# Two of the seven products of an opening block product cut by a third Strassen-Winograd step, with the routing projection's second quarter set between their pieces

## The chip, the cores and the metric

The kernel runs on one core of one Trainium2 chip. Its time is device time in microseconds (us). The program ran three times: 428.74, 428.77 and 429.66 us, median 428.77. One more execution was taken by the hardware profiler; every start and duration below is from that one. A difference of less than 0.2% (0.86 us) is not told apart from none.

TensorE (PE in the profile) multiplies matrices into PSUM. VectorE (DVE) adds and subtracts, ScalarE (ACT) copies, GpSimd (POOL) and SyncE (SP) hardly compute.

## The reference

All in float32. Layer 0 adds to `x` a dense product and a gated low-rank term, layer 1 adds a product with a weight matrix chosen by the row of the batch:

```python
# x: (8, 256, 1024)
base = einsum('btd,od->bto', x, W)                 # 1024 x 1024 weights
logits = einsum('btd,ed->bte', x, Wr) + bias       # 8 experts, +5 for the language's own
topw, topi = top_k(logits, 2)
gates = sum(one_hot(topi, 8) * softmax(topw)[..., None], -2)
h = einsum('btd,erd->bter', x, A)                  # 8 experts of rank 16
x = x + base + 2.0 * einsum('bter,bte,eor->bto', h, gates, B)
x = x + einsum('bsi,boi->bso', x, weight[adapter_ids])
```

The identity is added to the weight matrices, which makes the residual sums part of the products.

## The kernel before, in words

**Layer 0** is a product of 1024x1024 weights with 1024x2048 tokens, by two nested steps of the Strassen-Winograd scheme: seven block products instead of eight, each of which again is seven of eight smaller ones. A block product (keys "1" to "7") has weights `wb` and tokens `xb` of four quadrants each, `a(i, j)` (256x256) and `b(i, j)` (256x512). Its seven smaller products P1 to P7 need sums and differences of quadrants, made on DVE: `s1` to `s3` of the weights and `t1` to `t3` of the tokens; late in the product `s2` and `t2` are overwritten by a further difference (`late`). One smaller product is four matmuls of 128x128 weights with 128x512 tokens (`mm`, line 447), each of which is two records in the profile. Results gather in PSUM tiles A, B and X, and go out by an ACT copy or by a DVE sum onto what is there already (`evict`, line 435; every DVE sum and difference has line 217).

**A third step** exists in `product`, for its smaller product P2 alone: there, seven 128x256 matmuls (`deep`, line 513), called pieces here, stand for the four. Its own small sums are `r1` to `r4` (128x128) and `q1` to `q4` (128x256); `r1`, `r3` share a buffer, and so do `q1`, `q3`. Pieces 1, 6 and 7 are added up one after the other in one PSUM bank, and after each of them the bank's content is taken out; piece 5 has a bank of its own; pieces 2, 3 and 4 add straight onto a tile that gathers.

**PSUM**[...] three pairs (tags pair0, pair1, pair2) and two singles.

**The opening** is block product "1". It has a function of its own, `opening`, since it runs while inputs still arrive. Between its smaller products stand parts of the **projection** (`project`, line 245): tokens times the 136 columns of `A` and `Wr`, 32 matmuls of 128x136 for each of four quarters (two halves j of the tokens, two of each half c). The first quarter is (0, 0). A quarter is eight chunks, one for each 128 of the contraction, with four matmuls in each. `take` brings a quarter out: for each of two banks a DVE sum for the logits and an ACT copy for h.

The last smaller products of the opening are P7 (`mm(A, t["s3"], t["t3"])`), P3 (`mm(B, t["s2"], b(1, 1))`, onto B, then a DVE sum) and P4 (`mm(A, a(1, 1), t["t2"])`, onto A, then an ACT copy).

**The order around the change** is written out by hand[...]. After the opening, DVE makes differences of the low-rank B (`b_differences`), adds the identity to a weight block, makes two weight sums and `s1`, `s2` of product "5"; then comes the second quarter, `project(1, 0)`, and its take, four differences of x (`t1`), the third quarter `project(1, 1)` and its take, the gating of the half 1 (`gating`, some twenty small operations on DVE and one on ACT, last a product of the gates onto h), the other four differences of x, the fourth quarter `project(0, 1)`, the transposes of the gated h (`turn`, line 315), and product "5". Later products hand out DVE work between their matmuls from a list (`todo`, `pump`).

**Layer 1** handles eight batch rows, one adapter each, with one Strassen-Winograd step (`adapt`, line 660); loads of the weights run through SP's queue.

Of the kernel before, what the change touches and what calls it, by code (L numbers as in the profile page):

```python
# [25 lines left out]
def kernel(  # L26
# [335 lines left out]
        return pieces(fn, wb[out_], wb[x], wb[y], 2)  # L362

    subs = {}

    def make_subs(key, w, x, further=True):

        def a(i, j):  # L370
            return wb[w][:, 2 * j : 2 * j + 2, i * OQ : (i + 1) * OQ]

        def b(i, j):
            return xb[x][:, 2 * i : 2 * i + 2, j * TQ : (j + 1) * TQ]


        ra = lambda i, j: a(0, 1)[:, j, ts(i, P)]
        rb = lambda i, j: b(1, 0)[:, i, ts(j, TQ // 2)]
        t = {}

        def op3(name, tag, fn, x, y, first=4):
            width = P if name[0] == "r" else TQ // 2

            def run():
                t[name] = sub3.tile([P, width], F32, name=f"{name}_{key}", tag=tag)
                fn(t[name], *(t[v] if isinstance(v, str) else v for v in (x, y)))

            return us(width), first, run

        deep = [  # L390
            op3("r1", "r13", add, ra(1, 0), ra(1, 1)),
            op3("q1", "q13", minus, rb(0, 1), rb(0, 0)),
            op3("r2", "r2", minus, "r1", ra(0, 0)),
            op3("q2", "q2", minus, rb(1, 1), "q1"),
            op3("r4", "r4", minus, ra(0, 1), "r2"),
            op3("q4", "q4", minus, rb(1, 0), "q2"),
        ]

        def deep3():
            for o in (  # L400
                op3("r3", "r13", minus, ra(0, 0), ra(1, 0)),
                op3("q3", "q13", minus, rb(1, 1), rb(0, 1)),
            ):
                o[2]()

        def op(name, fn, x, y, first):
            pool = sub2 if name[1] == "2" else sub1
            width = OQ if name[0] == "s" else TQ

            def run():  # L410
                t[name] = pool.tile([P, 2, width], F32, name=f"{name}_{key}", tag=name)
                fn(t[name], *(t[v] if isinstance(v, str) else v for v in (x, y)))

            return us(2 * width), first, run

        def late_s():
            minus(t["s2"], a(0, 1), t["s2"])

        def late_t():
            minus(t["t2"], b(1, 0), t["t2"])  # L420

        subs[key] = (a, b, t, (late_s, late_t), (ra, rb, deep3), further)
        return [
            op("s1", add, a(1, 0), a(1, 1), 3),
            op("t1", minus, b(0, 1), b(0, 0), 3),
            op("s2", minus, "s1", a(0, 0), 3),
            op("t2", minus, b(1, 1), "t1", 3),
            op("s3", minus, a(0, 0), a(1, 0), 5),
            op("t3", minus, b(1, 1), b(0, 1), 5),
        ] + (deep if further else [])  # L430

    def evict(dest, acc, base=None):

# [24 lines left out]
    def opening(key, dest):  # L458


        idle = pair("idle", 2)
        for i in range(WARM):
            nc.tensor.matmul(idle[:, 0, :P], lhsT=ident, rhs=ident, start=True, stop=True)  # L463
        mm = multiply()
        sums_of = make_subs(key, "11", "11", False)
        a, b, t, late, _, _ = subs.pop(key)
        X = pair(f"X_{key}", 0)
        A = pair(f"A_{key}", 1)
        add_identity(wb["11"], 0, 2)
        mm(X, a(0, 1), b(1, 0), True, part=(0,))  # L470
        project(0, 0, singles("ps_h_0_0"), (2,), last=False)
        mm(X, a(0, 1), b(1, 0), part=(1,))
        evict(dest[:, 0], X)
        project(0, 0, None, (3,), False, False)
        mm(A, a(0, 0), b(0, 0), True, part=(0,))
        project(0, 0, None, (0,), False, False)
        mm(A, a(0, 0), b(0, 0), part=(1,))
        project(0, 0, None, (1,), False, False)
        use_adapter_ids()
        add_identity(wb["11"], 2, 4)  # L480
        for s in sums_of[:4]:
            s[2]()
        add(dest[:, 0], A, dest[:, 0])
        nc.tensor.matmul(idle[:, 1, :NB], lhsT=ones, rhs=ids_f[:, :NB], start=True, stop=True)
        use_ids(idle[:, 1, :NB])
        B = pair(f"B_{key}", 2)
        mm(B, t["s1"], t["t1"], True)
        evict(dest[:, 3], B)
        for s in sums_of[4:]:
            s[2]()  # L490
        mm(A, t["s2"], t["t2"])
        evict(dest[:, 1], A)
        project(0, 0, None, range(KH, KC), False)
        take(0, 0)
        for f in late:
            f()
        mm(A, t["s3"], t["t3"])
        add(dest[:, 3], A, dest[:, 3])
        mm(B, t["s2"], b(1, 1))
        add(dest[:, 1], B, dest[:, 1])  # L500
        mm(A, a(1, 1), t["t2"])
        evict(dest[:, 2], A)

    def product(key, base, dest, lora=None, tokens=None):

        a, b, t, late, (ra, rb, deep3), further = subs.pop(key)
        mm = multiply(dict(zip("01d", b_part(lora))) if lora is not None else None, tokens)
        new = roles(key)
        old = [base[:, q] if base is not None else None for q in range(4)]
        n0, n1 = (slice(j * (TQ // 2), (j + 1) * (TQ // 2)) for j in range(2))  # L510

        def deep(acc, lhs, rhs, first=False):
            nc.tensor.matmul(acc, lhsT=lhs, rhs=rhs, start=first, stop=True, skip_group_check=True)  # L513

        def quarter(m, n):

            return dest[:, 0][:, m, n], old[0][:, m, n] if base is not None else None

        A = new("A")
        mm(A, a(0, 0), b(0, 0), True)  # L520
        X = new("X")
        nc.scalar.copy(X, A)
        if not further:
            pump(1)
            B = new("B")
            mm(B, t["s1"], t["t1"], True, "1", 1)
            evict(dest[:, 3], B, old[3])
            pump(3)
            mm(A, t["s2"], t["t2"])
            evict(dest[:, 1], A, old[1])  # L530
            pump(3)
            mm(X, a(0, 1), b(1, 0), False, "0", 0)
            late[0]()
            late[1]()
            evict(dest[:, 0], X, old[0])
            pump(4)
            mm(A, t["s3"], t["t3"])
            add(dest[:, 3], A, dest[:, 3])
            pump(5)
            mm(B, t["s2"], b(1, 1), False, "d", 1)  # L540
            add(dest[:, 1], B, dest[:, 1])
            pump(6)
            mm(A, a(1, 1), t["t2"], False, "1", 0)
            evict(dest[:, 2], A, old[2])
            pump(7)
            return
        A3 = single(f"A3_{key}", 0)[:, n0]
        deep(A3, ra(0, 0), rb(0, 0), True)
        q, o = quarter(0, n0)
        evict(q, A3, o)  # L550
        pump(1)
        B = new("B")
        mm(B, t["s1"], t["t1"], True, "1", 1, ms=(0,))
        B3 = single(f"B3_{key}", 1)[:, n0]
        deep(B3, t["r1"], t["q1"], True)
        deep3()
        mm(A, t["s2"], t["t2"])
        evict(dest[:, 1], A, old[1])
        deep(A3, t["r2"], t["q2"])
        q, o = quarter(0, n1)  # L560
        evict(q, A3, o)
        late[0]()
        pump(2)
        mm(B, t["s1"], t["t1"], True, "1", 1, ms=(1,))
        evict(dest[:, 3], B, old[3])
        late[1]()
        pump(3)
        deep(X[:, 0, n0], ra(0, 1), rb(1, 0))
        deep(X[:, 0, n1], t["r4"], rb(1, 1))
        deep(X[:, 1, n0], ra(1, 1), t["q4"])  # L570
        mm(X, None, None, False, "0", 0, part=())
        deep(A3, t["r3"], t["q3"])
        two = [P, 2, TQ // 2]
        d1 = dest[:, 0][:, 1, :].rearrange("p (j n) -> p j n", j=2)
        both = A3.unsqueeze(1).to_broadcast(two)
        evict(d1, both, old[0][:, 1, :].rearrange("p (j n) -> p j n", j=2) if base is not None else None)
        add(dest[:, 0][:, :, n1], B3.unsqueeze(1).to_broadcast(two), dest[:, 0][:, :, n1])
        add(dest[:, 0], X, dest[:, 0])
        pump(4)
        mm(A, t["s3"], t["t3"])  # L580
        add(dest[:, 3], A, dest[:, 3])
        pump(5)
        mm(B, t["s2"], b(1, 1), False, "d", 1)
        add(dest[:, 1], B, dest[:, 1])
        pump(6)
        mm(A, a(1, 1), t["t2"], False, "1", 0)
        evict(dest[:, 2], A, old[2])
        pump(7)
# [176 lines left out]
    subs5 = make_subs("5", "21", "12")  # L765
    subs5[0][2]()
    subs5[2][2]()
    project(1, 0, halves(pair("ps_h_1_0", 0)))
    take(1, 0)

    def t1(c, k):
# [102 lines left out]
```

## Time and profile before

| | |
|---|---|
| median of three runs | 428.77 us |
| the profiled execution's own time | 430.16 us |
| its span (first to last instruction) | 428.4 us |
| PE busy | 423.1 us, 99%, 1246 records |
| weight loads (PEld) | 217.3 us, 51% |
| DVE busy | 281.7 us, 66%, 375 instructions |
| ACT busy | 39.6 us, 9%, 65 instructions |
| granted TensorE clock | 0.999 of full speed |
| DMA | 55.83 MB, mean 130 GB/s |
| P3 of the opening starts on PE | 31.48 us |
| second quarter of the projection starts on PE | 38.34 us |
| transposes start on PE | 60.58 us |

A line of the timeline has the start, the length from the first start to the last end, engine, source line, operation, the tile written, the tiles read, their shape and how many instructions are merged in it. Brackets give how long the engine had been idle, and what ended that. Where instructions are merged, the time of one follows from the difference of two starts rather than from a record's length, since matmul records overlap. A tile's name in the profile is that of the buffer: `y` holds the results and, early on, also the logits, gates and h; `x`, `w` are inputs; `s`, `t`, `r`, `q` the sums.

### The profile page before, as it was taken

Reading aid. Unit: us, or ns where it says so; the run is one execution under the profiler, and the core shown is the slowest. Engines: PE = TensorE matmul, PEld = TensorE weight load, DVE = VectorE, ACT = ScalarE, POOL = GpSimd, SP = SyncE. Lnnn points to the kernel's source line nnn. Section 1 sums busy time; section 2 is a strip of 40 time slices with the busy share of each in tenths; the row PEclk is TensorE's granted clock in tenths of the full one; section 3 lists DMA queues with packets and bytes.
Section 4 is the critical chain, followed back from the end, with each engine's and each line's share of the span. In section 5 each row is a group of like instructions: output and inputs, shape, how many; then the busy total and the mean of one; then the engine's idle time right before and its main releaser. Section 6 shows DMA issues by size and latency. Waiting matters only on the chain.

```text
span 428.4 us, 3335 instructions
## 1 busy us (share of the span) xinstructions
PE 423.1 (99%) x1246; PEld 217.3 (51%) x1246; DVE 281.7 (66%) x375; ACT 39.6 (9%) x65; POOL 2.0 (0%) x10
## 2 busy tenths in 40 slices
PE   8999999999999999999999999999999999999996
PEld 5566984545444445444454444444444444444574
DVE  1627288956988959889595676565756576565531
ACT  1120022110000000000000101010110101010110
POOL 1000000000000000000000000000000000000000
PEclk9999999999999999999999999999999999999999
DMA  8995000000000140630302276556748385550202
GB/s 279 383 398 217 2 0 2 0 0 2 0 0 0 31 168 0 249 142 0 99 0 98 98 262 227 199 207 208 272 148 313 128 275 214 196 197 0 98 2 99
DMA packets 14305, 55.83 MB, mean 130 GB/s; under 512 B 1232, under 2 KB 3536, under 8 KB 9808
## 3 DMA queue, kind: packets, MB, share of 16 engines
q1 hardware_dynamic: 12976, 54.68, 35.5%
q10 hardware_dynamic: 1248, 0.93, 0.7%
q8 instruction: 10, 0.16, 0.2%
q14 instruction: 7, 0.06, 0.0%
q0 software_dynamic: 64, 0.00, 0.0%
HBM read 47.22 MB, written 8.39 MB: 130 GB/s over the span
## 4 chain that ended last, share of the span: by engine, by line
PE 98%; DVE 0%; POOL 0%; issue 0%; ACT 0%; POOLq 0%; DVEq 0%
PE A L447 24%; PE A L660 22%; PE B L447 14%; PE B L660 13%; PE ps_h L245 7%; PE X L660 6%; PE X L447 4%; PE A_last L718 3%; PE A L513 1%; PE X L513 1%; PE idle L463 1%; PE ps_g L315 0%; PE B L513 0%; DVE y L217 0%; ACT z L748 0%
## 5 line engine op out<-in xcount | busy, mean ns | idle before, releaser
L660 PE MATMUL B<-x,x 128*128 128x512 f32 x128 | 57.5, 592 | 0.0
L447 PE MATMUL A<-t,s 128*128 128x512 f32 x112 | 50.3, 592 | 0.0
L217 DVE TENSOR_TENSOR y<-A,y 128x1024 f32<-128x1024 f32 (+2 forms) x27 | 26.3, 985 | 25.1 <-PE A L447 14.2
L660 PE MATMUL A<-w,x 128*128 128x512 f32 x88 | 39.6, 592 | 0.0
L660 PEld LDWEIGHTS B<-x,x 128*128 128x128 f32 x128 | 24.3, 190 | 29.8 <-issue 29.7
L217 DVE TENSOR_TENSOR w<-w,w 128x1024 f32<-128x1024 f32 x24 | 29.0, 1223 | 15.4 <-PE A L660 15.3
L660 PE MATMUL A<-w,y 128*128 128x512 f32 x88 | 39.1, 592 | 0.0
L447 PEld LDWEIGHTS A<-t,s 128*128 128x128 f32 x112 | 21.2, 190 | 22.9 <-issue 22.5
L245 PEld LDWEIGHTS ps_h<-y,x 128*128 128x128 f32 x256 | 30.7, 191 | 3.3 <-issue 3.3
L245 PE MATMUL ps_h<-y,x 128*128 128x136 f32 x256 | 30.6, 279 | 0.0
L660 PEld LDWEIGHTS A<-w,x 128*128 128x128 f32 x88 | 16.7, 190 | 21.0 <-issue 21.0
L660 PEld LDWEIGHTS A<-w,y 128*128 128x128 f32 x88 | 16.7, 190 | 21.0 <-issue 21.0
L435 ACT COPY z<-A 128x512 f32<-128x512 f32 x21 | 12.3, 586 | 158.3 <-PE A L660 158.3
L447 PE MATMUL B<-t,s 128*128 128x512 f32 x56 | 25.9, 594 | 0.3 <-DVE bias L200 0.3
L447 PE MATMUL A<-x,w 128*128 128x512 f32 x56 | 25.3, 592 | 0.0
L447 PE MATMUL A<-t,w 128*128 128x512 f32 x56 | 25.2, 592 | 0.0
L447 PE MATMUL B<-x,s 128*128 128x512 f32 x56 | 25.2, 592 | 0.0
L217 DVE TENSOR_TENSOR y<-B,y 128x1024 f32<-128x1024 f32 (+1 forms) x16 | 17.4, 1090 | 9.5 <-PE B L447 8.7
L217 DVE TENSOR_TENSOR x<-x,x 128x1024 f32<-128x1024 f32 (+1 forms) x20 | 19.2, 1004 | 0.0
L447 PEld LDWEIGHTS B<-x,s 128*128 128x128 f32 x56 | 10.6, 190 | 13.4 <-issue 12.7
L447 PEld LDWEIGHTS A<-t,w 128*128 128x128 f32 x56 | 10.6, 190 | 13.4 <-issue 12.7
L217 DVE TENSOR_TENSOR z<-X,z 128x512 f32<-128x512 f32 x8 | 5.5, 692 | 17.9 <-PE X L660 15.9
(119 smaller groups left out, 446.3 us busy)
## 6 DMA issues: line engine op xcount, KB each, us to landing
x<-w_dram SPq DMA_DIRECT2D x24, 1024.0 KB, 4.8
w<-w_dram SPq DMA_DIRECT2D x8, 1024.0 KB, 4.8
out_dram<-z SPq DMA_DIRECT2D x15, 512.0 KB, 3.0
x<-xT_dram SPq DMA_DIRECT2D x6, 1024.0 KB, 12.9
w<-wT_dram SPq DMA_DIRECT2D x3, 1024.0 KB, 14.9
x<-xT_dram SPq DMA_DIRECT2D x4, 256.0 KB, 3.8
x<-xT_dram SPq DMA_DIRECT2D x2, 512.0 KB, 7.4
w<-w11T_dram SPq DMA_DIRECT2D x1, 512.0 KB, 6.1
```

Source lines behind the costliest of these rows:

```text
L217: nc.vector.tensor_tensor(out_, x, y, op)
L245: nc.tensor.matmul(ps[v][:, u * EA : (u + 1) * EA], lhsT=xk(k, j, c)[:, ts(r, P)], rhs=aw_sb[:, k, :], start=(first and k == some[0] and u ...
L435: nc.scalar.copy(dest, acc)
L447: nc.tensor.matmul(acc[:, m, :], lhsT=l, rhs=r, start=(first and i < len(ms)), stop=(i >= len(steps) - len(ms)), skip_group_check=True,)
L463: nc.tensor.matmul(idle[:, 0, :P], lhsT=ident, rhs=ident, start=True, stop=True)
L513: nc.tensor.matmul(acc, lhsT=lhs, rhs=rhs, start=first, stop=True, skip_group_check=True)
L660: nc.tensor.matmul(accs[name], lhsT=lhs[:, k // 2, k % 2, :], rhs=rhs[:, k, :], start=(first and k == 0), stop=(k == KH - 1), skip_group_c ...
L718: nc.tensor.matmul(acc, lhsT=lhs[:, k // 2, k % 2, :], rhs=rhs[:, k, ts(v, m)], start=(first and k == 0), stop=(k == KH - 1), skip_group_c ...
```

## The change

The code of the third step moves out of `make_subs` and `product` into one function, `third`, which gives back the small sums, the late small sums (`ops3`), a function for a piece and one for taking a bank out (`take`, called `out` in the opening). `product` uses it and keeps its order of work. In `opening`, P3 and P4 are each cut into seven pieces. The second quarter of the projection moves from behind the weight sums into the opening: its eight chunks stand between the pieces. P3's results are added by DVE onto the quadrant that is there; P4's pieces 1, 6 and 7 are copied by ACT, its piece 5 and the tile A are added by DVE, where P4 was one ACT copy before. P3's first small sums stand before the second late difference (`t2`) on DVE. The pieces use the two single banks, the quarter uses pair0.

```diff
+    def third(key, lhs, rhs):
+        ra = lambda i, j: lhs()[:, j, ts(i, P)]
+        rb = lambda i, j: rhs()[:, i, ts(j, NQ)]
...
+        def ops3():
+            op("r3", "r13", minus, A(0, 0), A(1, 0))[2]()
+            op("q3", "q13", minus, B(1, 1), B(0, 1))[2]()
+
+        def piece(n, acc=None):
+            if n in (1, 5):
+                own[n] = single(f"P{n}_{key}", n // 5)[:, n0]
+            out_, l, r = {
+                1: lambda: (own[1], ra(0, 0), rb(0, 0)),
+                2: lambda: (acc[:, 0, n0], ra(0, 1), rb(1, 0)),
+                3: lambda: (acc[:, 0, n1], t["r4"], rb(1, 1)),
+                4: lambda: (acc[:, 1, n0], ra(1, 1), t["q4"]),
+                5: lambda: (own[5], t["r1"], t["q1"]),
+                6: lambda: (own[1], t["r2"], t["q2"]),
+                7: lambda: (own[1], t["r3"], t["q3"]),
+            }[n]()
+            nc.tensor.matmul(out_, lhsT=l, rhs=r, start=(n in (1, 5)), stop=True, skip_group_check=True)
+
+        def take(n, dest, base=None):
+            cut = lambda v: {1: v[:, 0, n0], 6: v[:, 0, n1], 5: v[:, :, n1]}[n]
+            if n == 7:
+                cut = lambda v: v[:, 1, :].rearrange("p (j n) -> p j n", j=2)
+            src = own[5 if n == 5 else 1]
+            if n in (5, 7):
+                src = src.unsqueeze(1).to_broadcast([P, 2, NQ])
+            evict(cut(dest), src, None if base is None else cut(base))
...
     def opening(key, dest):
...
         take(0, 0)
-        for f in late:
-            f()
+        late[0]()
+        ops, ops3, piece, out = third(f"{key}b", lambda: t["s2"], lambda: b(1, 1))
+        for o in ops:
+            o[2]()
+        late[1]()
         mm(A, t["s3"], t["t3"])
         add(dest[:, 3], A, dest[:, 3])
-        mm(B, t["s2"], b(1, 1))
+        quarter = halves(pair("ps_h_1_0", 0))
+        chunk = lambda k: project(1, 0, quarter, (k,), k == 0, k == KC - 1)
+        chunk(0)
+        piece(1)
+        out(1, dest[:, 1], dest[:, 1])
+        piece(5)
+        ops3()
+        chunk(1)
+        piece(6)
+        out(6, dest[:, 1], dest[:, 1])
+        chunk(2)
+        for n in (2, 3, 4):
+            piece(n, B)
+        chunk(3)
+        piece(7)
+        out(7, dest[:, 1], dest[:, 1])
+        last_out = out
+        ops, ops3, piece, out = third(f"{key}a", lambda: a(1, 1), lambda: t["t2"])
+        for o in ops[:2]:
+            o[2]()
+        last_out(5, dest[:, 1], dest[:, 1])
+        for o in ops[2:]:
+            o[2]()
         add(dest[:, 1], B, dest[:, 1])
-        mm(A, a(1, 1), t["t2"])
-        evict(dest[:, 2], A)
+        chunk(4)
+        piece(1)
+        out(1, dest[:, 2])
+        chunk(5)
+        piece(5)
+        ops3()
+        chunk(6)
+        piece(6)
+        out(6, dest[:, 2])
+        for n in (2, 3, 4):
+            piece(n, A)
+        chunk(7)
+        piece(7)
+        out(7, dest[:, 2])
+        out(5, dest[:, 2], dest[:, 2])
+        add(dest[:, 2], A, dest[:, 2])
...
     subs5[2][2]()
-    project(1, 0, halves(pair("ps_h_1_0", 0)))
     take(1, 0)
```

More of the change, by code (lines that the diff above doesn't have):

```diff
@@ L364, with op, run @@
     subs = {}
+    NQ = TQ // 2
+    def third(key, lhs, rhs):
+        ra = lambda i, j: lhs()[:, j, ts(i, P)]
+        rb = lambda i, j: rhs()[:, i, ts(j, NQ)]
+        n0, n1 = slice(0, NQ), slice(NQ, TQ)
+        t, own = {}, {}
+        def op(name, tag, fn, x, y):
+            width = P if name[0] == "r" else NQ
+            def run():
+                t[name] = sub3.tile([P, width], F32, name=f"{name}_{key}", tag=tag)
+                fn(t[name], *(t[v] if isinstance(v, str) else v() for v in (x, y)))
+            return us(width), 4, run
+        A, B = (lambda i, j: lambda: ra(i, j)), (lambda i, j: lambda: rb(i, j))
+        ops = [
+            op("r1", "r13", add, A(1, 0), A(1, 1)),
+            op("q1", "q13", minus, B(0, 1), B(0, 0)),
+            op("r2", "r2", minus, "r1", A(0, 0)),
+            op("q2", "q2", minus, B(1, 1), "q1"),
+            op("r4", "r4", minus, A(0, 1), "r2"),
+            op("q4", "q4", minus, B(1, 0), "q2"),
+        ]
+        def ops3():
[22 more added lines that the diff above has]
+            evict(cut(dest), src, None if base is None else cut(base))
+        return ops, ops3, piece, take
     def make_subs(key, w, x, further=True):
@@ L374, in b @@
             return xb[x][:, 2 * i : 2 * i + 2, j * TQ : (j + 1) * TQ]
-        ra = lambda i, j: a(0, 1)[:, j, ts(i, P)]
-        rb = lambda i, j: b(1, 0)[:, i, ts(j, TQ // 2)]
         t = {}
[L381 to L404, printed above, removed]
         def op(name, fn, x, y, first):
@@ L420, in late_t @@
             minus(t["t2"], b(1, 0), t["t2"])
-        subs[key] = (a, b, t, (late_s, late_t), (ra, rb, deep3), further)
+        deep = third(key, lambda: a(0, 1), lambda: b(1, 0)) if further else None
+        subs[key] = (a, b, t, (late_s, late_t), deep)
         return [
@@ L429, in make_subs @@
             op("t3", minus, b(1, 1), b(0, 1), 5),
-        ] + (deep if further else [])
+        ] + (deep[0] if further else [])
     def evict(dest, acc, base=None):
@@ L465, in opening @@
         sums_of = make_subs(key, "11", "11", False)
-        a, b, t, late, _, _ = subs.pop(key)
+        a, b, t, late, _ = subs.pop(key)
         X = pair(f"X_{key}", 0)
@@ L494, in opening @@
         take(0, 0)
-        for f in late:
-            f()
+        late[0]()
[3 more added lines that the diff above has]
+        late[1]()
         mm(A, t["s3"], t["t3"])
         add(dest[:, 3], A, dest[:, 3])
-        mm(B, t["s2"], b(1, 1))
-        add(dest[:, 1], B, dest[:, 1])
-        mm(A, a(1, 1), t["t2"])
-        evict(dest[:, 2], A)
+        quarter = halves(pair("ps_h_1_0", 0))
[21 more added lines that the diff above has]
+            o[2]()
+        add(dest[:, 1], B, dest[:, 1])
+        chunk(4)
[14 more added lines that the diff above has]
+        add(dest[:, 2], A, dest[:, 2])
     def product(key, base, dest, lora=None, tokens=None):
-        a, b, t, late, (ra, rb, deep3), further = subs.pop(key)
+        a, b, t, late, deep = subs.pop(key)
         mm = multiply(dict(zip("01d", b_part(lora))) if lora is not None else None, tokens)
@@ L509, in product @@
         old = [base[:, q] if base is not None else None for q in range(4)]
[L510 to L517, printed above, removed]
         A = new("A")
@@ L522, in product @@
         nc.scalar.copy(X, A)
-        if not further:
+        if deep is None:
             pump(1)
@@ L546, in product @@
             return
[L547 to L550, printed above, removed]
+        _, ops3, piece, take = deep
+        piece(1)
+        take(1, dest[:, 0], old[0])
         pump(1)
@@ L553, in product @@
         mm(B, t["s1"], t["t1"], True, "1", 1, ms=(0,))
-        B3 = single(f"B3_{key}", 1)[:, n0]
-        deep(B3, t["r1"], t["q1"], True)
-        deep3()
+        piece(5)
+        ops3()
         mm(A, t["s2"], t["t2"])
         evict(dest[:, 1], A, old[1])
-        deep(A3, t["r2"], t["q2"])
-        q, o = quarter(0, n1)
-        evict(q, A3, o)
+        piece(6)
+        take(6, dest[:, 0], old[0])
         late[0]()
@@ L567, in product @@
         pump(3)
-        deep(X[:, 0, n0], ra(0, 1), rb(1, 0))
-        deep(X[:, 0, n1], t["r4"], rb(1, 1))
-        deep(X[:, 1, n0], ra(1, 1), t["q4"])
+        for n in (2, 3, 4):
+            piece(n, X)
         mm(X, None, None, False, "0", 0, part=())
[L572 to L577, printed above, removed]
+        piece(7)
+        take(7, dest[:, 0], old[0])
+        take(5, dest[:, 0], dest[:, 0])
         add(dest[:, 0], X, dest[:, 0])
```

## The prediction

> **What bounds the kernel now.** I read the chain that ended last first. Each entry is a share of the span by engine:
>
> ```profile
> PE 98%; DVE 0%; POOL 0%; issue 0%; ACT 0%; POOLq 0%; DVEq 0%
> ```
>
> TensorE is the bound everywhere, so a matmul taken out is worth its pitch, unless TensorE then waits for something that had been in time. So next the busy time by stretch: from the sixth block product of the opening to the end of the projection's second quarter (27.93 to 45.68), then the two quarters up to the transposes. The columns are length, PE, PEld, DVE, ACT, POOL:
>
> ```profile
> 27.93:45.68 17.75, 17.75 (x91) 12.01 (x90) 10.34 (x15) 1.76 (x3) 0.00 (x0) 1.00 0.56 229
> 45.68:60.47 14.79, 14.79 (x131) 14.79 (x130) 8.59 (x30) 1.70 (x5) 0.00 (x0) 1.00 0.01 2
> ```
>
> PE has no gap in either; VectorE (DVE) is some six tenths busy. Whether that free time is where the change needs it, only the timeline tells (start, length, then the operation):
>
> ```profile
> 28.34 0.68 DVE L217 TENSOR_TENSOR s<-w,s 128x512 f32<-128x512 f32 x1
> 28.93 1.22 DVE L217 TENSOR_TENSOR t<-x,t 128x1024 f32<-128x1024 f32 x1
> 31.48 3.60 PE L447 MATMUL B<-x,s 128*128 128x512 f32 x8
> 31.75 1.23 DVE L217 TENSOR_TENSOR y<-A,y 128x1024 f32<-128x1024 f32 x1 [1.59 <-PE A L447]
> 34.91 3.60 PE L447 MATMUL A<-t,w 128*128 128x512 f32 x8
> 36.25 1.35 DVE L217 TENSOR_TENSOR bdiff<-b_sb 128x512 f32<-128x512 f32 x3
> 41.70 0.69 DVE L217 TENSOR_TENSOR s<-s,w 128x512 f32<-128x512 f32 x1
> 45.96 0.17 DVE L217 TENSOR_TENSOR y<-ps_h,bias 128x16 f32<-128x16 f32 x1 [3.57 <-PE ps_h L245]
> 46.66 2.49 DVE L217 TENSOR_TENSOR x<-x,x 128x512 f32<-128x512 f32 x4
> 53.37 0.17 DVE L217 TENSOR_TENSOR y<-ps_h,bias 128x16 f32<-128x16 f32 x1 [4.22 <-PE ps_h L245]
> 58.72 1.22 DVE L217 TENSOR_TENSOR y<-y,y 128x1024 f32<-128x1024 f32 x1
> 60.58 1.04 PE L315 MATMUL ps_g<-ident,y 128*128 128x128 f32 x8
> 75.20 0.59 PE L513 MATMUL X<-x,r 128*128 128x256 f32 x2
> 75.63 0.59 PE L513 MATMUL X<-q,w 128*128 128x256 f32 x2
> ```
>
> Three things are in it. A 128x512 product of four matmuls (eight records) has a pitch of 34.91 - 31.48 = 3.43 us; a 128x256 matmul (two records) one of 75.63 - 75.20 = 0.43. DVE has just two long waits before the transposes, 3.57 and 4.22 us, both for the projection. And its last operation before the transposes, the gates onto h (58.72), ends at 59.94; the transposes need it and start at 60.58. That is the slack of the stage: about 0.5 us.
>
> [...] DVE sat 1.59 us before the sum at 31.75 with nothing taken from behind it. [...] the first 128x512 records, from 4.25, are 0.86 us apart instead of 0.43, and are quick only after 7.7[...].
>
> **The change, part by part.**
> 1. TensorE. Two products of 3.43 become 2 x 7 x 0.43 = 6.02: 6.86 - 6.02 = 0.84 to 0.86 us less (0.86 with the finer 0.2145 per record). The 32 projection matmuls are only moved; a chunk is 8 records, 0.92 us (22.2 us for 192). No DMA issue moves, on SP's, ACT's or POOL's queue. Chunk 0 goes from 38.34 to 31.48; the last x load was issued at 16.2 and the slowest landed 14.5 after issue, so by 30.7 all are there.
> 2. New DVE work, by rows of the same shape: 128x128 0.29, 128x256 0.42, 128x512 0.69, 128x1024 1.23. An operation that depends on the one before starts 0.04 after its end, another 0.09 before it (62.44 to 63.57 after a 1.22). Eight small sums per product take 1.6 + 0.5; P3 adds four sums from PSUM (0.42, 0.42, 0.69, 0.69), P4 has three ACT copies (0.38, 0.38, 0.59) and one 0.69 on DVE; and what was one ACT copy after P4 (1.01) becomes copy, DVE sum, and a DVE sum of 1.23.
> 3. The order, walked through (P1 to P7 are pieces of P3, P1' to P7' of P4). A matmul's result is seen 0.38 + 0.11 us after its last record starts (0.38 is the length of a 128x256 record; the take at 45.96 shows 0.11 after such an end). DVE: s2 still ends at 29.02, six small sums run to 30.67, t2 follows, and the sum onto quarter 3 starts at 31.80 for 31.75: no harm. PE: chunk 0 at 31.48, P1 32.40, P5 32.83, chunk 1 33.26. P1 is seen at 33.10 and out of its bank at 33.53, so P6, which adds onto the same bank, is free to go when PE comes to it at 34.18. DVE makes the two small sums of P7 by 34.15 and takes P6 out from 34.88 to 35.31. PE: chunk 2 34.61, three pieces 35.53, chunk 3 36.82, P7 37.74, chunk 4 38.17. P7 goes out from 38.44 to 39.13. P4's first piece could start at 39.09, but it takes that bank: about 39.30, 0.2 lost, with all of PE's work behind it. DVE: two small sums to 39.92, P5 out 39.83 to 40.52, four small sums, B's sum at 41.50, the two small sums of P7' done at 43.25. PE: chunk 5 39.73, P5' 40.65 (its bank is free at 40.58), chunk 6 41.08, P6' 42.00 (its operands at 41.1, ACT's copy of P1' ended by 40.4), three pieces 42.43, chunk 7 43.72, P7' 44.64, the next quarter 45.07. Before it was 45.68: 0.6 us gained so far. The small sums cost nothing as long as DVE waits for PE here; uncovered they would be 4.2 us for both products.
> 4. What is late next. P7' is seen at 45.34; ACT copies it to 45.93; DVE's sum of P5' runs 45.97 to 46.66, that of A 46.70 to 47.93. Only then comes bdiff, at 47.84 for 36.25: 11.59 us later. Behind it in DVE's queue stand 6.05 us of differences and weight sums (36.25 to 42.39, less 0.09), the take of the quarter, four x differences, the second take and the gating. In before, they were there early. The two waits swallow 3.57 + 4.22 and twice the 0.09; so the gates onto h end 11.59 - 7.97 = 3.62 later, at 63.56. With 0.14 for the restart the transposes start at 63.70, not 60.58: 3.12 us late. PE is there at 59.97 and stands idle 3.7 us; the 0.6 gained is inside this wait, and isn't subtracted again.
> 5. After it. DVE is only 0.5 us later against PE than before. The next operands have more room: t1 of the product ends 63.66 and was needed at 65.11; later DVE itself waits for PE (1.10 us at 71.97), which evens it out. From there on PE is full to the end, so the 3.12 stays. ACT's copies fall into idle time (it waited 9.7 us at 38.54); without that cover they would be worth 1.35.
>
> Sum against the profiled execution: 428.4 + 3.12 = 431.5 of span. Its own time is 430.16, 1.8 above its span and 1.4 above the median of 428.77; I put the difference on the median: 431.9.
>
> **Rivals.**
> - *DVE's lateness is hidden, the matmuls count.* For it: DVE is idle 40% of this stretch, and PE is 98% of the chain. The price is -0.65 (with the lost 0.2) to -0.86: 427.9 to 428.1, not slower. It decides if the gates end by 59.8, that is if bdiff starts by 36.25 + 7.86 = 44.1. Against it: the A sum, which can't start before P7' (seen at 45.34) is out, stands before bdiff in the same queue. 3 in 100.
> - *The idle stretch makes the clock drop.* [...] 20 in 100.
> - *The hand-over of the two single banks is slower than walked.* P1' is already late, P5' has 0.07 to spare, and each tenth of PE's delay delays P7', hence bdiff, by as much. Four hand-overs at 0.05 to 0.25: 432.1 to 432.9, overlapping the forecast. Against it: P6 and P6' have over 0.6 of room. 10 in 100.
> - *The chain is shorter than I make it*, say a take that no longer waits its 0.44 for ACT: 429.6 to 431.2. 4 in 100.
>
> **How the numbers follow.** The forecast, 431.9, has 63 in 100, and its own range is 431.2 to 432.6, from some 0.05 on each of a dozen hand-overs. Bounds of the unknown: the restart of PE costs 0.05 (only the semaphore) to 0.3; I took 0.14, from the rows at 17.36, where PE had waited for DVE. [...] The range from 431.0 to 433.9 takes in the forecast, the slow hand-over[...]. A measurement tells 0.2%, 0.86 us, from no change. Only the hidden case lies about there: faster 0.02, same 0.03; slower 0.95.
>
> **What would show it.** Right: one idle stretch of TensorE of 3 to 4 us before the first transposes, ended by DVE's product onto h; bdiff near 47.8; DVE with no wait for the projection between; the next quarter's first matmul near 45.1 with at most some tenths of idle before P1'. A clock drop shows as 0.86 us pitch just after the transposes. Wrong: transposes at or before 60.6, or bdiff before the sum of A, or a second stretch of idle PE later than 65 us.

## The result, and the profile after

| | before | changed |
|---|---|---|
| median, in one comparison on one chip | 429.11 us (4 runs) | 433.31 us (4 runs) |
| ratio, with its 95% interval | | 1.0100 (1.0087 to 1.0113) |
| span of the profiled execution | 428.4 us | 431.3 us |
| its own time | 430.16 us | 433.08 us |

The change makes the kernel 1.0% slower, about 4.2 us. The two profiled executions differ by 2.9 us, less than the medians do. So there are two things to explain: the 2.9 us, and why the medians are further apart.

The chain that ended last, by engine, in the changed kernel. Before, TensorE held 98% of it and DVE nothing:

```profile
PE 94%; DVE 4%; ACT 0%; issue 0%; POOL 0%; DVEq 0%; POOLq 0%
```

The changed kernel's timeline, with the lines that answer to those shown of before (start, length, engine, source line, operation):

```profile
27.86 3.60 PE L479 MATMUL A<-t,s 128*128 128x512 f32 x8
32.22 0.59 PE L411 MATMUL P_1b<-x,s 128*128 128x256 f32 x2
34.01 0.60 PE L411 MATMUL P_1b<-q_1b,r_1b 128*128 128x256 f32 x2
38.02 1.09 PE L245 MATMUL ps_h<-y,x 128*128 128x136 f32 x8
38.97 0.70 PE L411 MATMUL P_1a<-t,w 128*128 128x256 f32 x2
39.51 1.09 PE L245 MATMUL ps_h<-y,x 128*128 128x136 f32 x8
40.43 0.59 PE L411 MATMUL P_1a<-q_1a,r_1a 128*128 128x256 f32 x2
44.45 0.59 PE L411 MATMUL P_1a<-q_1a,r_1a 128*128 128x256 f32 x2
44.88 14.99 PE L245 MATMUL ps_h<-y,x 128*128 128x136 f32 x128
63.51 1.06 PE L315 MATMUL ps_g<-ident,y 128*128 128x128 f32 x8 [3.64 <-DVE y L217]
...
39.37 0.68 DVE L217 TENSOR_TENSOR y<-P_1b,y 128x512 f32<-128x512 f32 x1
42.37 0.42 DVE L217 TENSOR_TENSOR q_1a<-t 128x256 f32<-128x256 f32 x1
45.70 0.69 DVE L217 TENSOR_TENSOR y<-P_1a,y 128x512 f32<-128x512 f32 x1 [2.90 <-ACT y L467]
46.49 1.23 DVE L217 TENSOR_TENSOR y<-A,y 128x1024 f32<-128x1024 f32 x1
47.63 1.35 DVE L217 TENSOR_TENSOR bdiff<-b_sb 128x512 f32<-128x512 f32 x3
53.69 0.17 DVE L217 TENSOR_TENSOR y<-ps_h,bias 128x16 f32<-128x16 f32 x1
54.30 0.17 DVE L217 TENSOR_TENSOR y<-ps_h,bias 128x16 f32<-128x16 f32 x1 [0.44 <-ACT y L262]
56.79 0.17 DVE L217 TENSOR_TENSOR y<-ps_h,bias 128x16 f32<-128x16 f32 x1
62.14 1.22 DVE L217 TENSOR_TENSOR y<-y,y 128x1024 f32<-128x1024 f32 x1
```

In the first half TensorE goes through pieces and chunks nearly without a gap. Then it stands idle for 3.64 us before the transposes, until DVE has put the gates onto h. DVE's two takes of the projection start without a bracket now (53.69 and 56.79): where DVE waited 3.57 and 4.22 us for TensorE before, it now comes late. Its last long wait is the 2.90 us at 45.70, for ACT's copy of P4's seventh piece. bdiff stands behind that and the sum of A: it starts at 47.63, though what it reads was there by 36.25 in the kernel before.

Starts can't be compared directly between executions, because the opening's length varies. The first four 128x512 records take 3.46 us in the profile of before and 1.83 in that of e3, so the projection matmuls behind them start at 7.71 and 6.21 us; the other profiles lie between. From there to P7 it is 20.3 us in all nine. So I cut each profiled execution in three: up to the first matmul of the opening's P7 (I), from there to the first transpose (II), and from the transposes to the end of the span (III). The experiments are those of the next section.

| profile | I | II | III |
|---|---|---|---|
| before | 28.04 | 32.54 | 367.8 |
| changed | 27.86 | 35.65 | 367.8 |
| changed, again (e0) | 27.75 | 35.64 | 370.3 |
| last two sums later (e1) | 27.11 | 31.84 | 367.8 |
| P4 whole (e2) | 28.00 | 32.12 | 367.8 |
| before, DVE late (e3) | 26.54 | 35.29 | 369.5 |
| chunks alone (e4) | 26.77 | 32.54 | 367.8 |
| changed, DVE later still (e5) | 27.83 | 39.29 | 370.2 |
| changed, TensorE kept busy (e6) | 27.98 | 35.65 | 367.8 |

Stage II holds all of the 3.11 us between before and changed. Stage III is 367.8 in six of the nine, and 1.7 to 2.5 more in three. The 2.9 of the profiled spans is the 3.11 of stage II, less the 0.18 by which the opening was shorter.

### The profile page after: what moved, and what is told of

It is laid out like the page before. It is cut to its first block, busy times and chain, and to the rows that moved or that the text cites. A ratio compares the mean times of both kernels' runs of the same rounds, so it can differ in the third digit from the quotient of the medians.

```text
span 431.3 us, 3384 instructions
## 1 busy us (share of the span) xinstructions
PE 422.4 (98%) x1258; PEld 219.7 (51%) x1258; DVE 289.9 (67%) x397; ACT 40.0 (9%) x67; POOL 2.0 (0%) x10
## 4 chain that ended last, share of the span: by engine, by line
PE 94%; DVE 4%; ACT 0%; issue 0%; POOL 0%; DVEq 0%; POOLq 0%
PE A L479 23%; PE A L716 22%; PE B L479 14%; PE B L716 13%; PE X L716 6%; PE X L479 4%; PE ps_h L245 3%; PE A_last L774 3%; DVE y L217 2%; PE P L411 2%; PE X L411 1%; DVE w L217 1%; PE idle L495 1%; DVE x L217 1%; PE ps_g L315 0%; PE P_1a L411 0%
## 5 line engine op out<-in xcount | busy, mean ns | idle before, releaser
L245 PEld LDWEIGHTS ps_h<-y,x 128*128 128x128 f32 x256 | 31.8, 190 | 3.6 <-issue 3.1
L217 DVE TENSOR_TENSOR y<-A,y 128x1024 f32<-128x1024 f32 x19 | 23.2, 1223 | 15.2 <-PE A L479 15.1
L245 PE MATMUL ps_h<-y,x 128*128 128x136 f32 x256 | 31.9, 279 | 0.0
L479 PE MATMUL B<-x,s 128*128 128x512 f32 x48 | 21.6, 592 | 0.0
L479 PE MATMUL A<-t,w 128*128 128x512 f32 x48 | 21.6, 592 | 0.0
L217 DVE TENSOR_TENSOR y<-B,y 128x1024 f32<-128x1024 f32 x12 | 14.7, 1222 | 7.0 <-PE B L479 7.0
L217 DVE TENSOR_TENSOR t<-x 128x1024 f32<-128x1024 f32 x14 | 17.1, 1221 | 0.5 <-DMA x<-xT_dram 0.5
L217 DVE TENSOR_TENSOR t<-x,t 128x1024 f32<-128x1024 f32 x14 | 17.1, 1219 | 0.0
```

The lines of the kernel that those rows point to most:

```text
L217: nc.vector.tensor_tensor(out_, x, y, op)
L245: nc.tensor.matmul(ps[v][:, u * EA : (u + 1) * EA], lhsT=xk(k, j, c)[:, ts(r, P)], rhs=aw_sb[:, k, :], start=(first and k == some[0] and u ...
L479: nc.tensor.matmul(acc[:, m, :], lhsT=l, rhs=r, start=(first and i < len(ms)), stop=(i >= len(steps) - len(ms)), skip_group_check=True,)
```

## Experiments

e0, e1, e3 and e5 were timed on one chip beside the kernel before (429.35 us, 14 runs), e2, e4 and e6 on another (429.34 us, 27 runs). In the code, three dots stand for lines that are not shown.

**e1: the last two sums moved back in DVE's queue.** Is it their place ahead of bdiff?

```diff
         out(7, dest[:, 2])
-        out(5, dest[:, 2], dest[:, 2])
-        add(dest[:, 2], A, dest[:, 2])
+        return lambda: out(5, dest[:, 2], dest[:, 2]), lambda: add(dest[:, 2], A, dest[:, 2])
...
-    opening("1", y21)
+    rest = opening("1", y21)
...
     subs5[2][2]()
+    rest[0]()
     take(1, 0)
...
     for t in gating(1):
         t[2]()
+    rest[1]()
```

> The changed kernel with its last two DVE sums (P5' and the tile A onto quarter 2) moved back in DVE's queue: the first behind the weight sums and product 5's s1 and s2, the second behind the gating. All pieces and chunks stay. Theory (the sums, which wait for P7', hold up the queue): bdiff starts near 42.7 instead of 47.6, DVE waits for the projection again, the transposes start within 0.2 us after the projection ends, near 59.8, and the span is 0.6 to 0.7 us under that of before: 427.7 to 427.9, 3.5 below the changed kernel. Rival (pieces and chunks themselves cost TensorE the time, or DVE simply has too much work before the gates): an idle stretch of 2 us or more before the transposes stays and the span is 430 or more.

Measured: 428.57 us (10 runs) against 429.35 for before (14 runs), ratio 0.9980 (0.9971 to 0.9990). The difference of 0.78 us is small, but the interval lies below 1. Its timeline:

```profile
41.96 1.36 DVE L217 TENSOR_TENSOR bdiff<-b_sb 128x512 f32<-128x512 f32 x3
48.02 0.68 DVE L217 TENSOR_TENSOR y<-P_1a,y 128x512 f32<-128x512 f32 x1
57.09 1.22 DVE L217 TENSOR_TENSOR y<-y,y 128x1024 f32<-128x1024 f32 x1
58.24 1.22 DVE L217 TENSOR_TENSOR y<-A,y 128x1024 f32<-128x1024 f32 x1
58.95 1.04 PE L315 MATMUL ps_g<-ident,y 128*128 128x128 f32 x8
```

The gates end at 58.31, before the projection does, and the transposes follow with no idle stretch. With all pieces and chunks in place stage II is 31.84: 0.70 under before, 3.81 under the changed kernel. So the place of two sums in one queue decides between 1% slower and 0.2% faster, and this version is the fastest of the three.

**e4: the chunks moved, no pieces.**

```diff
-        mm(B, t["s2"], b(1, 1))
...
+        chunk(0)
+        mm(B, t["s2"], b(1, 1), part=(0,))
+        chunk(1)
+        chunk(2)
+        mm(B, t["s2"], b(1, 1), part=(1,))
         add(dest[:, 1], B, dest[:, 1])
-        mm(A, a(1, 1), t["t2"])
+        chunk(3)
+        chunk(4)
+        mm(A, a(1, 1), t["t2"], part=(0,))
+        chunk(5)
+        chunk(6)
+        mm(A, a(1, 1), t["t2"], part=(1,))
         evict(dest[:, 2], A)
+        chunk(7)
...
-    project(1, 0, halves(pair("ps_h_1_0", 0)))
```

> The kernel before with the second quarter's eight chunks set between the halves of P3 and P4, both of these as four 128x512 matmuls; no pieces, no new sums. Theory: the move costs nothing and brings nothing: bdiff 1.9 us later, swallowed; within 0.2 us of before, no idle stretch. Rival (the move of the projection holds up TensorE or DVE): 1 us or more over before.

Measured: ratio 0.9999 (0.9990 to 1.0008); stage II 32.54, as before to the hundredth. bdiff came 2.8 us later against P7 (37.76 - 26.77 instead of 36.25 - 28.04), not 1.9, and was swallowed all the same. The move by itself is free.

**e2: P3 in pieces, P4 whole.** P4's pieces, small sums and ways out are replaced (only the new lines are shown):

```diff
         chunk(4)
...
+        mm(A, a(1, 1), t["t2"], part=(0,))
         chunk(5)
...
+        mm(A, a(1, 1), t["t2"], part=(1,))
+        evict(dest[:, 2], A)
         chunk(6)
...
         chunk(7)
...
```

> P3 in pieces as in the changed kernel, P4 as four 128x512 matmuls with its ACT copy as before, the chunks set between. Theory (what costs is P4's way out, whose last sums wait for P7' and hold up DVE): bdiff starts near 40.7, 4.4 us later than before, which the 7.97 us of waits swallow; no idle stretch of TensorE; 0.43 us under before. Rival (moved chunks or pieces as such cost, P3's as well): an idle stretch of about half the changed kernel's, 1.5 us over before.

Measured: 428.92 us against 429.34, ratio 0.9996 (0.9986 to 1.0007), which alone would not tell a gain from none (one of its 14 runs, at 431.31 with a granted clock of 0.994, I can't explain). Stage II tells: 32.12, 0.42 under before. DVE waits for the projection again, 2.72 us at the second take:

```profile
40.95 1.35 DVE L217 TENSOR_TENSOR bdiff<-b_sb 128x512 f32<-128x512 f32 x3
52.91 0.17 DVE L217 TENSOR_TENSOR y<-ps_h,bias 128x16 f32<-128x16 f32 x1 [2.72 <-PE ps_h L245]
60.12 1.04 PE L315 MATMUL ps_g<-ident,y 128*128 128x128 f32 x8
```

P3 in pieces brings 0.42 and does no harm. The harm comes with P4 in pieces, and by e1 with the place of its last two sums.

**e3: the kernel before, with DVE made late and nothing else.**

```diff
     opening("1", y21)
+    pad = sub1.tile([P, 2, TQ], F32, name="pad", tag="t1")
+    for _ in range(9):
+        add(pad, xb["11"][:, 0:2, :TQ], xb["11"][:, 2:4, :TQ])
     b_differences()
```

> The kernel before with nine DVE sums of 128x1024 into a scratch tile ahead of bdiff, nothing else: 9 x 1.26 = 11.3 us of lateness for DVE alone, no pieces, no moved chunks. Theory (7.97 us of waits and about 0.5 of slack swallow the rest): transposes 11.3 - 8.5 = 2.8 us later, near 63.4, span 431.2. If DVE's lateness were hidden: 428.4. If the pieces cost the time: also 428.4.

Measured: 432.94 us (4 runs), ratio 1.0090 (1.0073 to 1.0106).

```profile
34.75 11.29 DVE L217 TENSOR_TENSOR pad<-x 128x1024 f32<-128x1024 f32 x9
61.83 1.35 PE L315 MATMUL ps_g<-ident,y 128*128 128x128 f32 x8 [2.58 <-DVE y L217]
```

The pad runs from 34.75 to 46.04 and stage II grows by 2.75 us, for 2.8 expected. Lateness of DVE alone, with P3 and P4 whole, gives nearly the changed kernel's loss. Its stage III is 1.7 longer, though, which I hadn't expected after an idle stretch of only 2.58 us. That the profiled span of 431.3 fits the expected 431.2 is luck: the opening was 1.50 shorter than in the profile of before, which hides most of the 1.7. Why stage III is longer, the clock shows.

**e0: the changed kernel again, and e5: with three such sums ahead of bdiff.**

> The changed kernel once more, in more rounds, since four runs of it stood 4.2 us above before while the two profiled spans differ by 2.9, and two of the four had a granted clock of 0.996. Theory (one idle stretch of 3.6 us, clock kept): 2.9 to 3.1 us over before, clock 0.999 in all. Rival (the idle stretch lets the clock drop in some executions[...]): clock 0.996 in a part of the runs and those 1 to 2 us longer than the others, the mean 3.5 to 4.5 over before.

> The changed kernel with three DVE sums of 128x1024 into a scratch tile ahead of bdiff: 3.8 us more lateness, an idle stretch of 7.4 us[...]. If the clock is kept: 3.8 us over the changed kernel, span 435.1, matmuls after the transposes at their usual pitch of 0.43. [...]

e0 measured 434.12 us (5 runs), ratio 1.0104 (1.0088 to 1.0120). The theory of a kept clock is out; the rival holds in kind, with a little more than it gave: 4.77 us over before instead of 3.5 to 4.5, and the runs with a lowered clock 1.1 to 2.8 us longer than the one without, instead of 1 to 2. With the four runs of the first table the changed kernel ran nine times: three runs had a granted clock of 0.999 and took 432.74 to 433.08, six had 0.992 to 0.996 and took 433.55 to 435.51. e0's profile is of one of these. In its busy time by stretch (length, PE, PEld, DVE, ACT, POOL, then granted clock, DMA share and GB/s) the clock is the third column from the end:

```profile
58.36:61.77 3.41, 1.40 (x13) 1.19 (x11) 2.76 (x16) 0.21 (x1) 0.00 (x0) 1.00 0.00 0
61.77:68.60 6.83, 5.21 (x13) 3.18 (x14) 6.80 (x13) 1.63 (x4) 0.00 (x0) 0.50 0.01 2
68.60:72.01 3.41, 3.41 (x11) 1.68 (x10) 3.34 (x10) 1.29 (x2) 0.00 (x0) 1.00 0.00 0
```

Half the clock from 61.77 to 68.60. The same shows in the timeline, where up to the next line the transposes take 1.73 us instead of 0.90 (63.51 to 64.41 in the profile above) and eight records of 128x512 take 5.17 instead of 3.43:

```profile
63.39 1.94 PE L315 MATMUL ps_g<-ident,y 128*128 128x128 f32 x8 [3.63 <-DVE y L217]
65.12 5.33 PE L479 MATMUL A<-x,w 128*128 128x512 f32 x8
70.29 0.59 PE L411 MATMUL P<-x,w 128*128 128x256 f32 x2
```

From the transposes on, 68.60 - 63.39 = 5.21 us of work at half speed lose 2.6: stage III's excess is 2.5. e5 measured 438.29 us (4 runs), ratio 1.0205 (1.0181 to 1.0229). Stage II grew by 3.64 us for 3.8 expected. The clock was not kept: all four runs had a lowered one, 0.988 to 0.992, and their spans, 437.3 (the profiled one), 437.6, 435.5 and 435.7, lie above the 435.1 of a kept clock. The last two are 1.8 and 1.6 under the profiled one. An opening as short as e3's, 1.3 us shorter, would be most of that, but there is no profile of these two.

**e6: TensorE kept busy in the idle stretch.**

```diff
     project(0, 1, singles("ps_h_0_1"))
+    warm = pair("warm", 0)
+    for _ in range(4):
+        nc.tensor.matmul(warm[:, 0, :], lhsT=ident, rhs=xb["11"][:, 0, :TQ], start=True, stop=True)
     turn(1, halves(pair("ps_g_1", 2)))
```

> The changed kernel with four 128x512 matmuls (identity times inputs, result not used) on TensorE between the projection and the transposes: 8 x 0.43 = 3.43 us of work inside an idle stretch of 3.6. Theory A (stall and clock are two terms): the transposes start as late as in the changed kernel, 18.6 us after the third quarter's first matmul, the clock stays at 0.999 or above in every run, and the time is 0.7 to 1.2 us under the changed kernel's median, 3.0 to 3.4 over before. Rival (no part of the changed kernel's time comes from the clock): same time as the changed kernel, 4.2 to 4.8 over before, the spread of its runs unchanged.

```profile
59.82 3.60 PE L840 MATMUL warm<-x,ident 128*128 128x512 f32 x8
63.63 1.06 PE L315 MATMUL ps_g<-ident,y 128*128 128x128 f32 x8 [0.21 <-DVE y L217]
64.53 3.60 PE L479 MATMUL A<-x,w 128*128 128x512 f32 x8
```

Measured: 432.89 us (5 runs), ratio 1.0075 (1.0060 to 1.0090). That is 1.2 under e0, at the upper end of theory A's 0.7 to 1.2; but it is 3.55 over before, where theory A gave 3.0 to 3.4 and the first table has 4.20. The intervals of e6 and e0 still overlap a little, so the clock is the firmer sign: it was 0.999 or 1.0 in all five runs, against three of nine without the extra matmuls, and the five times, 432.32 to 433.20, lie about those of the three. Stage II is the changed kernel's 35.65. With work whose result nobody uses the runs with a lowered clock are gone, and their longer times with them. The stall itself stays.

## Why the prediction was right, and where not

**The mechanism and its size: right.** Stage II grew by 3.11 us; the working had 3.12.

*Point 1, TensorE's gain.* 0.42 for one product (e2) and 0.70 for both (e1) where 0.43 and 0.86 less 0.2 stood; the chunks' move costs nothing (e4).

*Point 3, the order.* The walk held at each hand-over on TensorE. (On DVE it adds up 0.28 too much from P7's way out on: with the 0.18 below, P5 goes out at 39.55, not 39.83. DVE waits for P7' after that, so nothing came of it.) The one stall is where it was put: 38.02 + 0.92 is 38.94, and from P1' to the next chunk it is 0.54 instead of 0.43, so some 0.14 are lost, not 0.2. P6 and P5' do not wait (34.01 and 40.43 have no bracket).

*Point 4, what is late next.* With 0.18 added for the shorter opening of this execution, bdiff is at 47.81 (working 47.84), the gates end at 63.54 (63.56), the transposes start at 63.69 (63.70). DVE swallowed its two waits as said. That the queue is the cause, and not the pieces, e1, e2 and e3 show from three sides: pieces without the queued sums are free of it, DVE's lateness without pieces has it.

*Point 5, after it.* Stage III is unchanged at 367.8, where the clock is kept. Where it is not, at 369.5 to 370.3, this step failed.

**The median: 1.4 us too low, inside the range.** 433.31 = 429.11 + 3.11 + 1.09, and the 3.11 is the stall of stage II. Of the miss, 0.3 is that the median of before was 429.11 in that comparison instead of 428.77. The 1.09 has two parts.

*The opening, about 0.8.* The two runs of the first table that kept their clock took 433.02 and 433.08, already 3.9 over the 429.11 of before, and e6 is 3.55 over with the clock kept in every run. So 0.8 of the 1.09, and 0.4 in e6, is no drop of the clock. The length of the opening explains it, by an estimate. In the profiles stages II and III take 403.4 us in the changed kernel and 400.4 in before. Taken off the spans of single runs they leave stage I: 27.8 and 27.9 us for the two runs, 27.7 for the median run of e6, but 27.2 for the median of the 27 runs of before beside e6 (26.4 to 27.9). The profiled execution of before, with its 28.04, lies above all of these, which is why the profiled spans differ by only 2.9. The step "I put the difference on the median" took the openings of both kernels' runs to be alike; in these few runs they were not. Whether the long openings of the changed kernel's runs are chance, or go together with a kept clock, stays open.

*The clock, the rest.* The median of 433.31 is 0.3 above the two runs that kept it; in e0, where four of five runs lost it, the median is 1.4 above the one that did not. Here the step that failed is the rival of the clock. I took it for a case of 20 in 100 that either holds or doesn't, and priced the forecast without it. It is a mixture: six of nine executions showed a lowered clock. Neither the 20 in 100 nor the room for a drop in the range's upper end, 433.9, rested on anything that the trace of before shows: between its first matmul and its last TensorE waits there for 0.32 us at most (at 17.37). By stage III a drop costs 1.7 to 2.5 us (e3, e5, e0).

The lowered stretches last about 3.4 us in e3 and 6.8 in e0 and e5. TensorE had not stood idle for as much as 3.4 us ahead of each of them: of the 3.41 us before the drop it was busy for 1.40 in e0 and for 0.82 in e3. What sets the three runs of the changed kernel that kept their clock apart from the six that did not, no run shows.

**The rivals.** Hidden lateness: wrong, as e3 shows. Slow hand-over of the banks: wrong, only 0.14 lost. A shorter chain: wrong; both takes keep their 0.44 (54.30 shows the first).

## What to carry to other kernels

When a step is cut finer, follow its last way out of PSUM to whatever stands behind it in that engine's queue, and add up the waits that could swallow the lateness; here 11.6 us of lateness met 8 us of waits. A sum that nobody needs soon belongs behind the work that somebody does: moving two of them turned 1% slower into 0.2% faster. A stall of TensorE of some 3 us cost more than its length in part of the runs here: behind stalls of 2.58 and 3.6 us the clock was lowered in two of four and six of nine, and stage III was 1.7 and 2.5 us longer in the two of these that were profiled. And before two profiled spans are compared, it helps to see where in the spread of its kernel's runs each of them lies.

## What was not expected of the hardware

Behind an idle stretch of only 2.58 us the clock was lowered too (e3, two of four runs: 0.996), and in the profiled one it fell near 62.4, after TensorE had restarted at 61.83. Busy time by stretch in e3, then in e5, cut at the ends of the lowered stretches and 3.41 us ahead of them:

```profile
58.96:62.37 3.41, 0.82 (x8) 0.65 (x7) 3.12 (x10) 0.09 (x1) 0.00 (x0) 1.00 0.00 0
62.37:65.79 3.42, 3.42 (x9) 1.87 (x8) 3.42 (x8) 1.64 (x4) 0.00 (x0) 0.51 0.00 0
```

```profile
58.25:61.66 3.41, 1.58 (x14) 1.38 (x12) 2.90 (x8) 0.99 (x3) 0.00 (x0) 1.00 0.00 0
61.66:65.07 3.41, 0.00 (x0) 0.00 (x0) 2.72 (x15) 0.21 (x1) 0.00 (x0) 1.00 0.00 0
65.07:71.90 6.83, 4.78 (x12) 3.11 (x13) 6.76 (x15) 1.63 (x4) 0.00 (x0) 0.51 0.01 2
```

TensorE's work in the lowered stretches prices the drops: half of 3.42 us is 1.7 for e3, half of 4.78 is 2.4 for e5, the same as stage III's excess in the table.

In the 3.41 us ahead of a lowered stretch TensorE was busy for 0.00 us in e5, 0.82 in e3 and 1.40 in e0. In e5 it was busy for 1.58 of the 3.41 us from 58.25, and the next 3.41 us had the full clock (1.00). How much work keeps the clock, these four stretches don't tell; no run here varied it on purpose. Why a lowered stretch lasts 3.4 us in e3 and 6.8 in e0 and e5 is not shown either; TensorE was busy for all 3.42 us of the one in e3, and for 5.21 and 4.78 of the 6.83 us in e0 and e5.
